# Seven inner products for two of the seven block products in a two-layer graph network

## The chip, the cores and the metric

The kernel runs on one core of one Trainium2 chip. A core has a matrix engine (TensorE, PE in the profile; its weight loads are PEld), three engines for elementwise work (VectorE or DVE, ScalarE or ACT, GpSimd or POOL), a queue engine (SyncE or SP) that issues the transfers, and 16 DMA engines. Every engine works through its own instructions in order; semaphores tie the engines together. The metric is the device time of one execution in microseconds. Before the change it is 2666.83 us, the median of three runs (2666.81 to 2668.23).

## What is computed

Two layers over 64 samples of 256 tokens with 512 features, in float32, all with the same 256x256 adjacency matrix:

```python
# layer 0: masked attention with 8 heads of 64, then residual and layer norm
q, k, v = x @ Wq + bq, x @ Wk + bk, x @ Wv + bv
scores = einsum('bqhd,bkhd->bhqk', q, k) / sqrt(64) + (1 - adj) * -1e9
x = layernorm(x + einsum('bhqk,bkhd->bqhd', softmax(scores), v) @ Wo + bo)
# layer 1: additive attention, then residual and layer norm
h = x @ W
e = leaky_relu((h @ a1)[:, :, None] + (h @ a2)[:, None, :], 0.2) * adj
x = layernorm(x + elu(softmax(e) @ h + beta * h))
```

## The kernel before

**Tiles.** The samples go in 32 pairs (`pair`, m = 0 to 31); q, k and v are made for both samples of a pair at once, all that follows for each sample s by itself (`batch`). Activations lie transposed, features on the 128 partitions, in four chunks of 128 features.

**Seven products.** A projection is cut into 2x2 blocks, and its eight block products are replaced by seven (Strassen's scheme in Winograd's form). `project` (line 435) issues them, in the order 1, 5, 2, 6, 3, 4, 7 for q, k and v of all pairs but the first. For q, k and v a block is 256 features by 256 features against 256 features by 256 tokens: four matmuls with 128x128 weights and 256 columns each. o and u have seven products of two such matmuls, spread (the second layer's attention times x) seven of two matmuls with 128 columns. The products gather in PSUM tiles (`ps_chain`, `ps_cross`, `ps_second`, `ps_fourth` or `ps_pair`); PSUM has eight banks. `gather` (line 490) brings them out: ScalarE copies the first product of a quarter (line 495, or 498 with a bias), VectorE adds the others onto it (line 504; for o, line 951).

**Sums of blocks.** The right-hand sums of tokens are GpSimd differences (`token_sums`, line 425; for spread, line 1083). Those of the weights are made once: for Wq and Wk by `streamed` (line 380), which puts them into DRAM and fetches each of the seven pieces again for every pair; for Wv, Wo and W they stay in SBUF (`weight_sums`, line 366).

**Attention.** `scores` (line 770) makes scores for two heads at a time, with 64-row weights, two matmuls side by side. VectorE adds the mask (line 786), ScalarE takes the exponential (line 788), GpSimd adds the two halves of the keys (line 791), VectorE transposes 32x32 blocks (line 797) and adds within them (line 798), which leaves four partial sums over keys. `denominators` (line 802) adds those four with one small matmul (`ps_den`, line 806), takes the reciprocal on VectorE (line 809), checks its range (line 811), and spreads it over all partitions through DRAM (lines 815 and 820). `mix` multiplies the weights with v, in two column halves (`ps_pv`, line 756); the result is divided on VectorE (line 873).

**Norm.** `norm` (line 584) takes the sum and the sum of squares on ScalarE (line 591), the root on GpSimd (lines 602 to 604), and scales on ScalarE (line 608). `finish` applies the elu on VectorE (lines 720 and 722).

**Order.** Nothing is issued where it is written. Each operation goes to a planner (`Plan`) with an assumed length, its buffers and what it reads and writes. TensorE's operations have a turn: `take_turn` (line 612) looks up the stage in `ROUND` and adds `LATER` to the pair's number, so that stages of several pairs interleave. The last pairs have an order written out, `FINISH`. `place` (line 127) keeps that order on TensorE and lays the other engines' operations by due time, with buffers counted in `slots`; it treats GpSimd and VectorE operations marked "two" as excluding each other. Every engine then runs the fixed order that results. In a middle period TensorE does: v, spread, scores, o, q, u, ps_den, mix, scores, k, spread, o, mix, ps_den, u.

## Time and profile before

| | |
|---|---|
| median of three runs | 2666.83 us |
| profiled execution | 2666.57 us |
| span of the profiled execution, first to last instruction | 2664.8 us |
| one period (a pair of samples) in the middle | 82.0 us |
| first matmul starts at | 3.75 us |
| last instructions behind the last matmul | 12.8 us |
| TensorE clock granted, mean | 0.998 of full speed |
| bytes from and to memory | 245.11 MB read, 52.48 MB written |
| DMA queue of the hardware, share of 16 engines | 42.1% |

In a row of the profile a line number says where the instruction stands in the kernel above, then come the engine, the operation, what it writes and reads, shapes (weights rows*columns for matmuls), and the count. A float32 matmul leaves two records. The lengths of matmuls are modelled; their starts are measured.

### The profile page before, as it was taken

The numbers are of one execution on the slowest core, as the hardware profiler recorded it, in microseconds if no ns is written. First come the engines' busy times: TensorE is split into PE (matmuls) and PEld (weight loads), VectorE is DVE, ScalarE is ACT, GpSimd is POOL, SyncE is SP. The second block draws the span as 40 slices with busy tenths as digits, with TensorE's granted clock in tenths as the row PEclk, the third lists the DMA queues.
The fourth block names the chain that finished last, engine by engine and source line by source line (L and its number), as shares of the span: only waits on it lengthen the run. The fifth ranks groups of instructions, "written<-read, shape, count | busy, mean of one in ns | idle before, by whom it ended". The sixth has DMA issues, their size and how long they took to land.

```text
span 2664.8 us, 45965 instructions
## 1 busy us (share of the span) xinstructions
PE 2643.7 (99%) x15037; PEld 2288.5 (86%) x15037; DVE 1999.7 (75%) x4053; ACT 1550.5 (58%) x3585; POOL 1637.5 (61%) x2255
## 2 busy tenths in 40 slices
PE   9999999999999999999999999999999999999998
PEld 7888888888888888888888888888888888888886
DVE  6677787777877777777778777787777777777876
ACT  3456565555655565655656555565556565565666
POOL 4665665655756556566566565575655656656655
PEclk9999999999999999999999999999999999999999
DMA  8343443444534434444344344453443444444321
GB/s 253 83 104 111 124 127 92 114 116 112 132 95 114 116 109 124 109 108 109 112 123 127 92 113 117 113 131 96 114 117 108 125 109 106 109 113 123 96 64 53
DMA packets 583084, 300.70 MB, mean 113 GB/s; under 512 B 409400, under 2 KB 513848, under 8 KB 582840
## 3 DMA queue, kind: packets, MB, share of 16 engines
q1 hardware_dynamic: 582712, 297.68, 42.1%
q8 instruction: 123, 2.02, 0.3%
q14 instruction: 121, 0.99, 0.1%
q0 software_dynamic: 128, 0.01, 0.0%
HBM read 245.11 MB, written 52.48 MB: 112 GB/s over the span
## 4 chain that ended last, share of the span: by engine, by line
PE 98%; DVE 0%; ACT 0%; DMA 0%; SPq 0%; issue 0%; POOL 0%; ACTq 0%; DVEq 0%
PE ps_chain L455 35%; PE ps_cross L455 23%; PE ps_sc L779 9%; PE ps_pv L756 9%; PE ps_pair L455 8%; PE ps_fourth L455 7%; PE ps_second L455 7%; PE ps_den L806 0%; DMA wq_sb<-in_L_gnn_Wq_dram 0%; ACT junk L591 0%; PE ps_plain L523 0%; DVE wq_sums_s L387 0%; DVE oT L873 0%; PE ps_y L1058 0%; PE ps_plain L518 0%; PE ps_plain L520 0%
## 5 line engine op out<-in xcount | busy, mean ns | idle before, releaser
L791 POOL TENSOR_TENSOR both<-pT 128x256 f32<-128x256 f32 x504 | 361.3, 742 | 55.9 <-ACT pT L788 55.8
L788 ACT ACTIVATE pT<-pT 128x512 f32<-128x512 f32 x512 | 307.0, 627 | 104.6 <-DVE pT L786 102.2
L602 POOL TENSOR_SCALAR rs<-sq 128x2 f32<-128x2 f32 (+1 forms) x130 | 25.4, 195 | 537.5 <-ACT junk L591 534.6
L591 ACT ACTIVATE junk<-x 128x512 f32<-128x512 f32 x256 | 159.7, 624 | 330.1 <-DVE x L951 311.8
L786 DVE TENSOR_TENSOR pT<-ps_sc,maskT_sb 128x512 f32<-128x512 f32 x512 | 319.7, 682 | 38.3 <-PE ps_sc L779 37.8
L1083 POOL TENSOR_TENSOR X_sums<-x 128x256 f32<-128x256 f32 x126 | 126.3, 1012 | 284.0 <-DVE x L720 211.6
L779 PE MATMUL ps_sc<-qT,kT 64*128 64x256 f32 x2048 | 240.2, 383 | 0.0
L756 PE MATMUL ps_pv<-pT,v 128*64 128x256 f32 x2048 | 238.1, 382 | 0.0
L779 PEld LDWEIGHTS ps_sc<-qT,kT 64*128 64x128 f32 x2048 | 193.2, 187 | 37.4 <-issue 12.2
L608 ACT ACTIVATE x<-x,nmr,rs 128x512 f32<-128x512 f32 x256 | 200.3, 807 | 31.5 <-POOL nmr L604 31.5
L756 PEld LDWEIGHTS ps_pv<-pT,v 128*64 128x64 f32 x2048 | 175.7, 137 | 44.3 <-issue 10.7
L974 DVE SCALAR_TENSOR_TENSOR junk<-x,wa_sb 128x512 f32<-128x512 f32 x256 | 173.9, 691 | 46.7 <-ACT x L608 46.6
L591 ACT ACTIVATE junk<-x,mean 128x512 f32<-128x512 f32 x256 | 182.8, 714 | 2.0
L797 DVE STREAM_TRANSPOSE flip<-both 128x512 f32<-128x512 f32 x252 | 176.8, 702 | 7.0 <-POOL both L791 0.5
L798 DVE TENSOR_REDUCE part<-flip 128x16 f32<-128x512 f32 x252 | 170.2, 676 | 3.2
L740 POOL TENSOR_TENSOR x<-x,res_sb 128x512 f32<-128x512 f32 x128 | 160.8, 1278 | 0.9 <-DMA x<-in_x_dram 0.9
L455 PE MATMUL ps_chain<-so_sb,oS 128*128 128x256 f32 x504 | 129.4, 379 | 0.0
L455 PE MATMUL ps_chain<-sw_sb,yS 128*128 128x256 f32 x504 | 129.4, 379 | 0.0
L951 DVE TENSOR_TENSOR x<-x,ps_chain 128x256 f32<-128x256 f32 x252 | 100.8, 411 | 28.9 <-PE ps_chain L455 27.8
L455 PE MATMUL ps_chain<-sv_sb,xS 128*128 128x256 f32 x512 | 120.9, 379 | 0.0
L425 POOL TENSOR_TENSOR oS<-oT 128x256 f32<-128x256 f32 x126 | 101.2, 803 | 30.8 <-DVE oT L873 23.1
L455 PE MATMUL ps_chain<-xS,wk_sums 128*128 128x256 f32 x496 | 117.2, 379 | 0.0
(246 smaller groups left out, 6985.2 us busy)
## 6 DMA issues: line engine op xcount, KB each, us to landing
x<-in_x_dram SPq DMA_DIRECT2D x64, 512.0 KB, 5.2
out_dram<-x SPq DMA_DIRECT2D x128, 256.0 KB, 2.9
inv_all<-rows SPq DMA_DIRECT2D x126, 256.0 KB, 4.1
xin<-in_x_dram SPq DMA_DIRECT2D x248, 128.0 KB, 3.2
wq_sums<-wq_sums SPq DMA_DIRECT2D x124, 256.0 KB, 3.4
wk_sums<-wk_sums SPq DMA_DIRECT2D x124, 256.0 KB, 2.6
wq_sums<-in_L_gnn_Wq_dram SPq DMA_DIRECT2D x93, 256.0 KB, 2.9
wk_sums<-in_L_gnn_Wk_dram SPq DMA_DIRECT2D x93, 256.0 KB, 2.7
```

The source lines that it names most:

```text
L455: nc.tensor.matmul(dst[:, f, :], lhs, rhs, start=start and f == 0 and c == 0, stop=c == inner - 1, skip_group_check=True)
L591: plan.op("ACT", ns, lambda: nc.scalar.activation(junk[A], X[:, t, :], func, accum_out=to[:, i:i + 1], **{k: v() if callable(v) else v for ...
L608: plan.op("ACT", 810, lambda i=i, t=t: nc.scalar.activation(X[:, t, :], X[:, t, :], AF.Identity, bias=nm[:, i:i + 1], scale=rs[:, i:i + 1] ...
L740: plan.op("POOL", 1300, lambda t=t: nc.gpsimd.tensor_tensor(X[:, t, :], X[:, t, :], res_sb[A], ALU.add), [res_sb], tokens(t))
L756: nc.tensor.matmul(acc[r * HD:(r + 1) * HD, i, :], V[:, 2 * k + s, h * HD:(h + 1) * HD], pT[h][:, k, :], start=k == 0, stop=k == NT - 1)
L779: nc.tensor.matmul(acc[j][:, k, :], kT[r:r + HD, c, key_blk(k)], own(qT, r, c), start=True, stop=True)
L786: plan.op("DVE", 680, lambda h=h, i=i: nc.vector.tensor_add(pT[h][A], acc[i][A], maskT_sb[A]), [acc[i], maskT_sb], [pT[h]])
L788: plan.op("ACT", 620, lambda h=h: nc.scalar.activation(pT[h][A], pT[h][A], AF.Exp, scale=1.0 / HD ** 0.5), [pT[h]], [pT[h]])
L791: plan.op("POOL", 735, lambda h=h, i=i: nc.gpsimd.tensor_tensor(both[c][:, i, :], pT[h][:, 0, :], pT[h][:, 1, :], ALU.add), [pT[h]], [(bot ...
L797: plan.op("DVE", 700, lambda: nc.vector.transpose(turned[A], both[c][A]), [both[c]], [turned])
L798: plan.op("DVE", 685, lambda: nc.vector.tensor_reduce(part[:, 2 * c:2 * c + 2, :], turned[A].rearrange("p i (q k) -> p i q k", k=32), AX.X ...
L974: plan.op("DVE", 770, lambda t=t, i=i, junk=junk: nc.vector.scalar_tensor_tensor(junk[A], X[:, t, :], 1.0, wa_sb[:, i, :], op0=ALU.mult, o ...
```

## The change

- **Inner products.** For all pairs but the first, products 2 and 4 of q, k and v are themselves cut into 2x2 blocks of 128x128 and made by seven matmuls with 128 columns, where there were four with 256. `inner_product` writes inner products 2, 3, 4 and 5 into the four quadrants of a PSUM tile, and 1, 6 and 7 into a second small one (`ps_inner`), to which 6 and 7 accumulate after the tile has been read. `add_part` adds the pieces to the quarters on VectorE: per product three additions of 128 columns and one of 256. `inner_sums` makes the token side of both, eight GpSimd differences of 128x128 a pair (`xQ`); the weight side is made once on GpSimd and streamed as two further pieces a projection.
- **Denominators.** The four partial sums come side by side by four DMAs, VectorE adds them (a reduction), takes the reciprocal of 64 columns and transposes it; the matmul goes, except for the last sample, which has its own.
- **Wv is streamed** like Wq and Wk, with nine buffers for pieces in place of six. In the first pair the token differences are on VectorE.
- **Order.** `ROUND`, `LATER` and `FINISH` are new, `START` writes out the first stages, k ahead of q; three matmuls on a constant stand first. A middle period on TensorE becomes: v, spread, o, u, k, mix, scores, q, spread, o, u, mix, scores.
- **Last pair.** The sum over features comes with the last addition of the elu (`accum_out`), and VectorE scales in ScalarE's place.

```diff
-ROUND = ("v", "x", "spread1", "scores20", "scores00", "scores10", "scores30", "o1", "logits0", "q", "logits1", "u1",
-         "sums0", "mix0", "scores11", "scores21", "scores01", "scores31", "attention0", "k", "spread0", "o0", "mix1",
-         "sums1", "u0", "attention1")
+ROUND = ("attention1", "v", "spread1", "attention0", "o1", "x", "u1", "k", "mix0", "scores01", "scores11", "scores21",
+         "scores31", "logits1", "q", "spread0", "o0", "u0", "logits0", "mix1", "scores00", "scores10", "scores20",
+         "scores30")
+LATER = {"scores00": -1, "scores10": -1, "scores20": -1, "scores30": -1, "scores01": 0, "scores11": 0, "scores21": 0,
+         "scores31": 0, "attention1": 2, "v": 0, "spread1": 2, "attention0": 1, "o1": 1, "x": -2, "u1": 2, "k": -1,
+         "mix0": 0, "logits1": 1, "q": -1, "spread0": 1, "o0": 0, "u0": 1, "logits0": 0, "mix1": 0}
...
+START = (("x", 0), ("k", 0), ("bias", 0), ("q", 0), ("x", 1), ("v", 0), ("mask", 0), ("scores10", 0), ("scores20", 0),
+         ("scores00", 0), ("scores11", 0), ("x", 2), ("scores30", 0), ("scores31", 0), ("mix0", 0), ("logits0", 0),
+         ("consts", 0), ("q", 1), ("scores21", 0), ("scores01", 0), ("v", 1), ("k", 1), ("mix1", 0), ("scores00", 1),
...
+DEEP = (2, 4)
...
-    slots = {"xin": 2, "x": 4, "two": 6, "xP": 1, "piece": 6, "full": 4, "half": 17, "flip": 1, "part": 1, "inv": 1,
-             "xS": 2, "st": 72, "ps": 8, "rows": 4, "svT": 4, "line": 4, "square": 4}
+    slots = {"xin": 2, "x": 4, "two": 6, "xP": 1, "piece": 9, "xQ": 2, "full": 4, "half": 19, "flip": 1, "part": 1, "inv": 1,
+             "xS": 2, "st": 72, "ps": 8, "rows": 4, "svT": 3, "line": 4, "square": 4}
...
+    busy(3)
...
+        inner = {}
+        for n in DEEP:
+            a = lambda f, c, n=n: w[:, 2 * raw[n][1] + c, (2 * raw[n][0] + f) * P:(2 * raw[n][0] + f + 1) * P]
+            I = sb("half", [4, P], f"{name}_i{n}")
+            for to, p, m, op, reads in (
+                    (0, (1, 0), (1, 1), ALU.add, [w]), (1, 0, (0, 0), ALU.subtract, [w, (I, 0)]),
+                    (2, (0, 0), (1, 0), ALU.subtract, [w]), (3, (0, 1), 1, ALU.subtract, [w, (I, 1)])):
+                plan.op("POOL", 455, lambda I=I, a=a, to=to, p=p, m=m, op=op: nc.gpsimd.tensor_tensor(
+                    I[:, to], *(a(*v) if isinstance(v, tuple) else I[:, v] for v in (p, m)), op), reads, [(I, to)])
...
+            if deep:
+                (raw_piece, reads), piece = fetch(n), sb("piece", [4, P], f"{name}_i{n}")
+                plan.op("SP", 370, lambda: nc.sync.dma_start(piece[A].rearrange("p k f -> p (k f)"), inner[n][A]),
+                        [inner[n]], [piece], lag=3900)
+                a = lambda f, c: (lambda: raw_piece()[:, c, blk(f)])
+                k = lambda i: (lambda: piece[:, i])
+                return [a(0, 0), a(0, 1), k(3), a(1, 1), k(0), k(1), k(2)], reads + [piece]
...
+            eng, ns = (nc.gpsimd, 180 + 545 * width // P) if engine == "POOL" else (nc.vector, 700)
+            plan.op(engine, ns, lambda: eng.tensor_tensor(dst(), p(), m(), ALU.subtract), reads, writes, mode="two")
...
+    def inner_sums(right, name):
+        r, keys = right
+        S = sb("xQ", [3, P], name)
+        b = lambda c, t: r()[:, c, t * P:(t + 1) * P]
+        ops = ((S, 2, (1, 1), (0, 1)), (None, (0, 1), (0, 1), (0, 0)), (S, 0, (1, 1), (0, 1)), (S, 1, (1, 0), 0))
+        for i, (buf, to, p, m) in enumerate(ops):
+            plan.op("POOL", 455, lambda to=to, p=p, m=m: nc.gpsimd.tensor_tensor(
+                *(b(*v) if isinstance(v, tuple) else S[:, v] for v in (to, p, m)), ALU.subtract),
+                keys + ([(S, 0)] if i == 3 else []), [(S, to)] if buf else keys)
+        b_, s_ = (lambda c, t: (lambda: b(c, t))), (lambda k: (lambda: S[:, k]))
+        return [b_(0, 0), b_(1, 0), b_(1, 1), s_(1), b_(0, 1), s_(0), s_(2)], keys + [S]
...
+        def inner_product(n, ks, to, start):
+            if n not in sums:
+                sums[n] = left(n, True)
+            reads = sums[n][1] + deep[n][1]
+            def pe():
+                for k in ks:
+                    f, t = {2: (0, 0), 3: (0, 1), 4: (1, 0), 5: (1, 1)}.get(k, (0, 0))
+                    l, r = sums[n][0][k - 1](), deep[n][0][k - 1]()
+                    dst = to[0][A] if to[0].shape == [P, P] else to[0][:, f, blk(t)] if by_feature else to[0][:, t, blk(f)]
+                    lhs, rhs = (l, r) if by_feature else (r, l)
+                    nc.tensor.matmul(dst, lhs, rhs, start=start and k == ks[0], stop=True, skip_group_check=True)
+            plan.op("PE", 224 * len(ks), pe, reads, [to], claims=claims)
+        def deep_four(n, whole, q, op):
+            inner_product(n, (2, 3, 4, 5), whole, True)
+            op(q, (whole, lambda: whole[0][A]))
+            add_part(q, (0, 1), (whole, lambda: whole[0][:, 1, P:2 * P]))
+            parts[n] = (ps([P], "ps_inner"), None)
+            inner_product(n, (1,), parts[n], True)
+            add_part(q, (0, 0), (parts[n], lambda: parts[n][0][A]))
+        def deep_six(n, q):
+            inner_product(n, (6,), parts[n], False)
+            add_part(q, (0, 1), (parts[n], lambda: parts[n][0][A]))
+        def deep_seven(n, q):
+            inner_product(n, (7,), parts[n], False)
+            add_part(q, (1, None), (parts[n], lambda: parts[n][0][A]))
+        if deep:
+            if 4 in deep:
+                deep_four(4, fourth, (1, 0), copy)
+            copy((0, 0), pe(1, chain, True))
+            if 2 in deep:
+                deep_four(2, second, (0, 0), add)
+            copy((1, 1), pe(5, cross, True))
+            if 4 in deep:
+                deep_six(4, (1, 0))
+            if 2 not in deep:
+                add((0, 0), pe(2, second, True))
+            copy((0, 1), pe(6, chain, False))
+            if 2 in deep:
+                deep_six(2, (0, 0))
+            if 4 in deep:
+                deep_seven(4, (1, 0))
+            add((0, 1), pe(3, cross, False))
+            if 4 not in deep:
+                copy((1, 0), pe(4, fourth, True))
+            if 2 in deep:
+                deep_seven(2, (0, 0))
+            acc = pe(7, chain, False)
+            add((1, 1), acc)
+            add((1, 0), acc)
+            return
...
+            def of():
+                return src() if t is not None else src().unsqueeze(1).to_broadcast([P, 2, P])
...
+            plan.op("DVE", 280 if t is not None else 410, both, [acc, key], [key])
...
+        if sums:
+            plan.op("DVE", 150, lambda: nc.vector.tensor_scalar(mean[A], sums[A], -1.0 / D, None, ALU.mult), [sums],
+                    [(mean, i) for i in range(n)])
...
+            if sums:
+                plan.op("DVE", 400, lambda i=i, t=t: nc.vector.tensor_scalar(
+                    X[:, t, :], X[:, t, :], rs[:, i:i + 1], nm[:, i:i + 1], ALU.mult, ALU.add),
+                    [nm, rs], [(X, (t, 0)), (X, (t, 1))], mode="two")
+                continue
...
+        elif (what, m) in START:
+            plan.turn = (-9, START.index((what, m)))
...
-        right = token_sums(xT, lambda k, j: [(xT, (j, s)) for s in range(2)], "xS", N)
+        right = token_sums(xT, lambda k, j: [(xT, (j, s)) for s in range(2)], "xS", N, "POOL" if m else "DVE")
+        deep = {n: inner_sums(right[n - 1], "xQ") for n in DEEP} if m else None
...
+            lv, left["v"] = streamed(wv_sb, Wv, "wv_sums")
...
-                turn("sums")
-                acc, inv = ps([32], "ps_den"), sb("inv", [32], "inv")
-                plan.op("PE", 80, lambda: nc.tensor.matmul(
-                    acc[0:P // 2], part[A].rearrange("p h q -> p (h q)"), fold_sb[A], start=True,
-                    stop=True), [part, fold_sb], [acc], mode="one", claims=[inv])
-                plan.op("DVE", 342, lambda: nc.vector.reciprocal(inv[0:P // 2], acc[0:P // 2]), [acc], [inv])
+                W, four = P // 4, sb("flip", [2, N], "four")
+                inv = sb("inv", [P // 2], "inv")
+                def gathered():
+                    return four[0:W, 0, :].rearrange("n (b c) -> n b c", b=4)
+                def fold():
+                    for b in range(4):
+                        nc.sync.dma_start(gathered()[:, b, :], part[b * W:(b + 1) * W].rearrange("n h q -> n (h q)"))
+                plan.op("SP", 1720, fold, [part], [(four, 0)], lag=2400)
+                plan.op("DVE", 330, lambda: nc.vector.tensor_reduce(
+                    inv[0:W], gathered().rearrange("n b c -> n c b"), AX.X, ALU.add), [(four, 0)], [inv])
+                plan.op("DVE", 200, lambda: nc.vector.reciprocal(inv[0:W], inv[0:W]), [], [inv])
                 for limit, op in ((SAFE, ALU.is_le), (1.0 / SAFE, ALU.is_ge)):
                     plan.op("DVE", 180, lambda limit=limit, op=op: nc.vector.scalar_tensor_tensor(
-                        fine_sb[0:P // 2], inv[0:P // 2], limit, fine_sb[0:P // 2], op0=op, op1=ALU.mult),
+                        fine_sb[0:W], inv[0:W], limit, fine_sb[0:W], op0=op, op1=ALU.mult),
                         [inv, fine_sb], [fine_sb], mode="two")
+                plan.op("DVE", 160, lambda: nc.vector.transpose(four[0:W, 1, 0:P // 2], inv[0:W]), [inv], [(four, 1)])
                 rows = Buf(dram_pool, "rows", [H, N], "rows")
                 plan.op("SP", 540, lambda: nc.sync.dma_start(
-                    rows[A].rearrange("h (q n) -> (h q) n", n=32), inv[0:P // 2]), [inv], [rows], lag=1700)
+                    rows[A].rearrange("h (q n) -> (h q) n", n=W).rearrange("(a j) n -> j a n", j=W),
+                    four[0:W, 1, 0:P // 2].rearrange("j (a n) -> j a n", n=W)), [(four, 1)], [rows], lag=1700)
...
```

## The prediction

> **What bounds the kernel now.** I read the page's busy shares and its chain of waits first, then TensorE's own timeline, then the busy time of every engine by stage.
>
> ```profile
> PE 2643.7 (99%) x15037; PEld 2288.5 (86%) x15037; DVE 1999.7 (75%) x4053; ACT 1550.5 (58%) x3585; POOL 1637.5 (61%) x2255
> PE 98%; DVE 0%; ACT 0%; DMA 0%; SPq 0%; issue 0%; POOL 0%; ACTq 0%; DVEq 0%
> ```
>
> TensorE is busy throughout, and 98% of the chain that ended last is TensorE's own work. A busy share alone would not do, since ends of matmuls are modelled; starts are not. So I take the price of a product from start to start. In the timeline (start, length, engine, line) the k products stand 1.73 us apart, the products of spread, half as wide, 0.45 us apart:
>
> ```profile
> 1045.94 1.89 PE L455 MATMUL ps_cross<-xT,wk_sums 128*128 128x256 f32 x8
> 1047.67 1.89 PE L455 MATMUL ps_second<-xT,wk_sums 128*128 128x256 f32 x8
> ...
> 1056.75 0.61 PE L455 MATMUL ps_cross<-attT,X_sums 128*128 128x128 f32 x4
> 1057.19 0.61 PE L455 MATMUL ps_second<-attT,x 128*128 128x128 f32 x4
> 1057.64 0.61 PE L455 MATMUL ps_chain<-att_sums,X_sums 128*128 128x128 f32 x4
> ...
> 1065.56 3.67 PE L756 MATMUL ps_pv<-pT,v 128*64 128x256 f32 x32
> 1069.07 0.25 PE L806 MATMUL ps_den<-fold_sb,part 128*64 128x32 f32 x2
> 1069.25 1.13 PE L455 MATMUL ps_chain<-w_sb,yT 128*128 128x256 f32 x4
> ```
>
> One 128x128 by 256 matmul (two records) costs 1.73/4 = 0.432 us, one with 128 columns 0.447/2 = 0.2235 us. Nothing stands between products, so a matmul taken out shortens the span, as long as nobody else becomes late. Busy time by stretch (start:end, length, then PE, PEld, DVE, ACT, POOL) shows who might: one whole period (a pair of samples) and, in it, a scores block and the o block after it.
>
> ```profile
> 1000.10:1082.10 82.00, 82.00 (x470) 71.32 (x469) 61.93 (x127) 48.38 (x112) 50.91 (x71) 1.00 0.42 113
> 1008.70:1012.40 3.70, 3.70 (x34) 3.05 (x33) 3.68 (x8) 1.56 (x3) 3.29 (x4) 1.00 0.74 119
> 1012.40:1018.50 6.10, 6.10 (x30) 5.41 (x29) 6.00 (x14) 3.35 (x6) 6.10 (x9) 1.00 0.67 105
> ```
>
> VectorE is full for 10 us after the scores and GpSimd nearly so, and TensorE still waits for neither: short backlogs are absorbed by spare PSUM banks. At the two ends of the run TensorE does wait; the largest wait is in the o product of the first sample (idle before it in brackets), with slow matmuls behind it:
>
> ```profile
> 89.72 2.00 PE L455 MATMUL ps_cross<-wo_sb,oT 128*128 128x256 f32 x4 [2.21 <-POOL oT L425]
> 91.52 1.89 PE L455 MATMUL ps_pair<-wo_sb,oT 128*128 128x256 f32 x4
> ```
>
> **The inner products.** In pairs 1 to 31 products 2 and 4 of q, k and v become seven products of 128x128 blocks with 128 columns. Before: 2 x 4 x 0.432 = 3.456 us a projection. After: 2 x 7 x 0.2235 = 3.129 us. That is 0.327 us, less than the eighth of 0.432 that the count of multiplications promises, because a narrow matmul costs more than half a wide one. 31 x 3 x 0.327 = **30.4 us** off TensorE.
>
> Here a rule of the Trainium skill speaks against the change: "TensorE: Matmul & The Clock Gate", section Back-to-back issue gap, says that in a stream of weight load and matmul pairs the spacing is set by both, about 81 ns a pass at 128 columns, where the stream alone would need 56. The row has two records 112 ns apart for one matmul, which at that page's rates are four passes of 56 ns. By the rule a narrow matmul would cost 0.324 us, fourteen of them 4.54 us, and the change would lose 31 x 3 x 1.08 = 100 us. Spread's products are the same shape and type, with new weights for every matmul, so I take the row.
>
> **Sums over keys, and the order.** The sums' matmul is small: in the rows above pv and ps_den together take 3.69 us from pv's start to u's. A pv block without one (at 2606.0 us, before the last sums' spread) takes 3.60, so it costs 0.08 us here, and by the same count 0.11 where it stands ahead of pv: 0.19 a pair. The new order puts pv and scores side by side twice a pair, where before one scores and one pv block stood alone: six changes of tile mode a period instead of seven, each 0.09 to 0.1 us (a 256-column record is followed after 0.31 us instead of 0.216). 32 x 0.19 + 31 x 0.095 = **9.0 us**. So a period falls from 82.0 to about 80.7 us.
>
> In exchange the denominators take four more DMAs out of SP's queue, a reduction, a longer reciprocal and a transpose. From scores to the mix that needs nothing of them and then to o lie more than half a period, some 40 us; two DMA round trips at the page's 1.7 to 4.1 us fit. Behind them in SP's queue stand weight pieces. SP issues some 20 more DMAs a pair (7 pieces of v, 6 inner pieces, 8 folds), at 0.3 to 0.7 us each about 10 us, on a queue that waits most of the time; the pieces' bytes add 13 x 256 KB to 9.3 MB a pair, DMA share from 0.42 to about 0.55. I cost both at nothing; if a piece came late, TensorE would wait for its landing, about 3 us.
>
> **VectorE and GpSimd.** Each inner-product pair of a projection adds six additions of 128 columns from PSUM and two of 256. A 128x512 one takes 682 ns, a 128x256 one 411, so 128 columns take about 276 (estimate by that slope). Per pair 18 x 0.276 + 6 x 0.411 = 7.4 us of durations; since back-to-back instructions overlap (512 x 682 ns of L786 are 319.7 us busy, 0.92), 6.8 us. The denominators add about 1.7 us: reciprocal of 64 columns 0.55 (344 ns for 32, 154 for 2), reduction 0.41, transpose 0.23, checks 0.44, against 0.72 a sample. 61.9 + 8.5 = 70.4 us of 80.7, 87%. GpSimd adds eight differences of 457 ns (median of att_sums), 3.7 us: 54.6 of 80.7, 68%.
>
> The mean hides a tight stage. By the order of instructions of the changed program, from a scores block to the end of the u after v (3.65 + 11.8 + 3.2 + 6.1 + 6.1 = 30.8 us) VectorE does 8 mask additions (5.5), 12 additions for v (2.7 + 2.5), 4 flips and 4 reductions (5.5), two oT (1.5), two L722 (1.5), L974, attT and svT (1.7), 16 additions for spread, o, u (6.6), denominators (1.2), two xT transposes (2.4) and L720 (1.4): 32.5 us, times 0.92 is 29.9, **97%**. The q half has about 27 of 34 us, so a backlog is paid back within the period. The skill's "SBUF — State Buffer", section SBUF: two separate sides, says the port pair is an exclusive lock between GpSimd and a VectorE instruction with two SBUF inputs. The trace agrees (L387 on VectorE 1628 ns in the crowded start, 694 alone), so the oT and L722 instructions of that stage can each be held for one GpSimd instruction, 0.73 us. By the rows alone VectorE just keeps up; with the lock taken against it four times it ends some 3 us late, and the second inner accumulation of v, which I find about 0.5 us early, would wait. TensorE's new waits: between nothing and 2 us a pair. Nearest is the scores-o stage shown above, 98% full and without a wait; I take 0.15 us a pair, **+5 us**.
>
> GpSimd's closest date is xS and xQ (one xS buffer): after v's last product it does 4 of 1.28, 7 of 0.73 and 7 of 0.457, about 13.5 us, and k needs them 15.3 + 0.45 us later. No two-input VectorE work lies in that window, so 2 us remain.
>
> **Start and end.** The written order moves the first o to where its sums are long done: the block that took 10.37 us takes 6.15, and 0.73 before it goes, **-4.9**. Three warm-up matmuls run while x is fetched; q's first product took 3.2 us instead of 1.73 partly for a slow clock: **-1.5** (0 to -2.5). The scores that waited 0.85 us for the transposes do no longer. Against that, the first k product now finds VectorE with four token differences, bv_wo and kT ahead of the weight sums, and GpSimd with 24 differences that hold the port: +3 (1 to 6). Six scores in a row with the mix at once behind them: ten mask additions of 0.682 and an exp of 0.63 end about 2 us after TensorE gets there, +2. New pieces are first written, then read: +1 (0 to 4). Together **-1.2**. At the end the sum over features comes with the last addition and normalizing is done on VectorE, so 0.81 us of L591 become about 0.15 and 0.81 us of L608 about 0.48 (L544): **-1.0** of the 12.8 us behind the last matmul.
>
> **Sum.** 2664.8 - 30.4 - 9.0 - 1.2 - 1.0 + 5 = 2628.2 us of span. The profiled execution took 2666.57, 1.8 more than its span, and the median is 2666.83, 0.3 above it: **2630 us**. Its own range is 2617 to 2644. A measurement can tell 0.2% (5 us) from no change.
>
> **Rivals.** (1) VectorE is late now and then: waits of 0.8 us a pair instead of 0.15 leave half the gain, about 2650. For it the 97%, against it the 98% above that cost nothing. (2) Slower: in the v stage VectorE and GpSimd hold each other up in every period, and v's inner accumulations wait 2 us: 31 x 2 = 62 us against a gain of 41.6, about 2687. It decides from 1.3 us a pair. For it that both engines gained work and lost time, and that its instructions stand in a fixed order, so that one held by the port holds all behind it; against it that a backlog under 1 us is hidden by banks. A gap of 2.2 us also cost 2 us of half-speed clock at 89.7 us; gaps this small did not. (3) Narrow matmuls behave as the rule says, 2630 + 130 = 2760: hardly with the row at hand. (4) The reduction of work is real but v's pieces arrive late and eat it: within 5 us of before.
>
> **Chances.** Likeliest 0.66; (1) 0.16; (4) 0.05; (2) 0.11 and (3) 0.01 on the slow side; a bigger gain, below 2615, 0.01. Faster 0.83, same 0.05, slower 0.12. The range that leaves out no more than two in ten runs from a little under the likeliest case's lower end to rival (1)'s upper end: 2615 to 2662.
>
> **What would show it.** Right: a period of about 80.7 us from one k block to the next; inner products' matmuls 0.2235 us apart; VectorE near 87% and GpSimd near 68% in a middle period; no ps_den but the last sample's; the o block of the first sample at 6.15 us. Wrong: TensorE gaps before inner accumulations released by VectorE's part additions or oT, gaps before k's first products released by GpSimd's xQ, gaps released by weight pieces, or a start longer than 5 us of waits.

## The result, and the profile after

The changed kernel takes **2694.43 us** (median of four runs, 2691.39 to 2697.82), where the kernel before took 2667.44 beside it (2666.81 to 2668.23). The ratio is 1.0101, with a 95% interval of 1.0084 to 1.0119: it is slower by 27 us, where 37 us faster was forecast. The time lies outside the range and on the other side.

The page of the changed kernel, its busy shares and the chain that ended last, by engine and by line:

```profile
PE 2628.0 (98%) x16033; PEld 2243.8 (83%) x16033; DVE 2210.2 (82%) x4942; ACT 1503.8 (56%) x3573; POOL 1743.7 (65%) x2519
PE 73%; DMA 10%; DVE 10%; SPq 3%; issue 3%; ACT 1%; POOL 0%; DVEq 0%; POOLq 0%; ACTq 0%
PE ps_chain L515 25%; PE ps_cross L515 15%; PE ps_pv L918 8%; PE ps_sc L941 7%; PE ps_pair L515 6%; PE ps_inner L545 4%; DMA four<-part 4%; PE ps_fourth L545 3%; PE ps_second L545 3%; SPq L974 2%; DMA wv_sums_i<-wv_sums 2%; DVE xT L809 1%; DVE pT L948 1%; PE ps_fourth L515 1%; DVE inv L977 1%
```

TensorE is busy 15.7 us less than before, and yet the span is 28.6 us longer. The chain, which was 98% TensorE's, now leaves it for a quarter of the time, and the largest name in it beside TensorE's is the denominators' transfer `four<-part` with its issue on SP (line 974); the reduction that reads it (line 977) is there too.

One period in the middle (start:end, length, then PE, PEld, DVE, ACT and POOL busy, clock, DMA share, GB/s) against the prediction's 80.7 us, 70.4 us of VectorE, 54.6 of GpSimd and a DMA share of 0.55:

```profile
1043.40:1126.20 82.80, 80.72 (x498) 69.27 (x497) 68.17 (x154) 46.37 (x113) 54.65 (x79) 1.00 0.57 153
```

The loads are as forecast; only the length isn't. The prices are too. At the end of this period, in TensorE's timeline, the inner products' matmuls stand 0.22 us apart:

```profile
1126.19 0.39 PE L545 MATMUL ps_fourth<-xS,wk_sums_i 128*128 128x128 f32 x2
1126.42 0.39 PE L545 MATMUL ps_inner<-xS,wk_sums 128*128 128x128 f32 x2
1126.64 1.68 PE L515 MATMUL ps_chain<-xT,wk_sums 128*128 128x256 f32 x7
```

So the time went between the instructions. Start to start on TensorE, in us per block, between 150 and 2500 us (the sum counts k, q, v once, the rest twice a pair, as the period does):

| | before, mean | after, median | after, mean |
|---|---|---|---|
| k, q, v together | 36.37 | 35.58 | 35.88 |
| spread | 3.17 | 3.13 | 3.28 |
| o | 6.14 | 6.05 | 6.29 |
| u | 6.14 | 6.45 | 6.73 |
| scores | 3.65 | 3.65 | 3.65 |
| pv, with the sums' matmul before | 3.70 | 3.60 | 3.63 |

In a pair where nothing is late the period is 80.62 us, as forecast; in the mean it is about 2.2 us more. More than half of that lies in u, which takes 6.09 us (mean of its two) in that undisturbed pair. Here is one u, as TensorE, SP and VectorE went through it (start, length, engine, line; in brackets the idle time before and its releaser):

```profile
1119.78 1.03 PE L515 MATMUL ps_chain<-sw_sb,yS 128*128 128x256 f32 x4
1120.64 1.03 PE L515 MATMUL ps_cross<-sw_sb,yT 128*128 128x256 f32 x4
1123.72 1.10 PE L515 MATMUL ps_pair<-w_sb,yS 128*128 128x256 f32 x4 [2.05 <-DVE four L984]
```

```profile
1107.97 1.33 SPq L453 DMA_DIRECT2D wk_sums<-wk_sums  x3
1109.40 0.38 SPq L900 DMA_DIRECT2D x<-in_x_dram  x1
1109.87 0.42 SPq L453 DMA_DIRECT2D wk_sums<-wk_sums  x1
1110.34 0.58 SPq L1170 DMA_DIRECT2D line<-svT  x1
1115.67 0.32 SPq L1172 DMA_DIRECT2D row<-line  x1
1116.08 2.50 SPq L974 DMA_DIRECT2D four<-part  x4
```

```profile
1113.19 0.66 DVE L960 TENSOR_REDUCE part<-flip 128x16 f32<-128x512 f32 x1
...
1117.39 0.75 DVE L1123 TENSOR_TENSOR x<-x,ps_chain 128x256 f32<-128x256 f32 x2 [0.44 <-PE ps_chain L515]
1119.99 0.59 DVE L977 TENSOR_REDUCE inv<-four 32x64 f32<-32x256 f32 x1 [1.84 <-DMA four<-part]
1120.51 1.22 DVE L809 STREAM_TRANSPOSE xT<-xin 128x1024 f32<-128x1024 f32 x1
1121.66 0.50 DVE L979 RECIPROCAL inv<-inv 32x64 f32<-32x64 f32 x1
1122.09 1.18 DVE L809 STREAM_TRANSPOSE xT<-xin 128x1024 f32<-128x1024 f32 x1
1123.20 0.37 DVE L623 TENSOR_TENSOR u<-ps_pair,u 128x256 f32<-128x256 f32 x1
```

Read it backwards. TensorE waits for the PSUM bank of `ps_pair`, whose last user is the addition `u<-ps_pair` at 1123.20. (The profile names `four` at line 984, which ends at that moment; but in all 29 such gaps the matmul starts 0.15 us behind the addition's end, also in the one where another instruction follows it.) That addition stands in VectorE's fixed order behind the reduction at line 977, and VectorE stood idle for 1.84 us in front of it; of TensorE's 2.05 us that is nearly all. The reduction waited for the four fold DMAs. Their data was there at 1113.85, but SP issued the first only at 1116.08, because in SP's own order `row<-line` stands ahead, and that one waited 4.75 us for `line` to land. `line` holds 1 KB, but SP had issued 1.5 MB just ahead of it, four pieces of weights of 256 KB each and 512 KB of x. The waits of the whole run, VectorE's at the reduction and TensorE's behind it (total, times, longest):

```profile
DVE inv L977 <- DMA four<-part: 51.1, 52, 3.1
PE ps_pair L515 <- DVE four L984: 25.0, 28, 2.1
```

This is a reading, not yet a cause. The experiments have to tell whether that stand is what costs the time, or whether VectorE is simply too full, or whether it is the new order as a whole.

### The profile page after: what moved, and what is told of

It reads as the page before. It is cut to its first block, busy times and chain, and to the rows that moved or that the text cites. A ratio compares the mean times of both kernels' runs of the same rounds, so it can differ in the third digit from the quotient of the medians.

```text
span 2693.4 us, 50162 instructions
## 1 busy us (share of the span) xinstructions
PE 2628.0 (98%) x16033; PEld 2243.8 (83%) x16033; DVE 2210.2 (82%) x4942; ACT 1503.8 (56%) x3573; POOL 1743.7 (65%) x2519
## 3 DMA queue, kind: packets, MB, share of 16 engines
q1 hardware_dynamic: 666184, 408.06, 56.1%
q14 instruction: 138, 1.13, 0.1%
## 4 chain that ended last, share of the span: by engine, by line
PE 73%; DMA 10%; DVE 10%; SPq 3%; issue 3%; ACT 1%; POOL 0%; DVEq 0%; POOLq 0%; ACTq 0%
PE ps_chain L515 25%; PE ps_cross L515 15%; PE ps_pv L918 8%; PE ps_sc L941 7%; PE ps_pair L515 6%; PE ps_inner L545 4%; DMA four<-part 4%; PE ps_fourth L545 3%; PE ps_second L545 3%; SPq L974 2%; DMA wv_sums_i<-wv_sums 2%; DVE xT L809 1%; DVE pT L948 1%; PE ps_fourth L515 1%; DVE inv L977 1%
## 5 line engine op out<-in xcount | busy, mean ns | idle before, releaser
L953 POOL TENSOR_TENSOR both<-pT 128x256 f32<-128x256 f32 x504 | 382.3, 781 | 66.7 <-ACT pT L950 64.4
L918 PEld LDWEIGHTS ps_pv<-pT,v 128*64 128x64 f32 x2048 | 141.8, 137 | 87.1 <-issue 22.2
L1255 POOL TENSOR_TENSOR X_sums<-x 128x256 f32<-128x256 f32 x126 | 99.5, 800 | 168.6 <-ACT x L757 81.1
L757 ACT ACTIVATE x<-x,nmr,rs 128x512 f32<-128x512 f32 x252 | 194.7, 809 | 7.8 <-POOL nmr L748 6.2
L1146 DVE SCALAR_TENSOR_TENSOR junk<-x,wa_sb 128x512 f32<-128x512 f32 x256 | 192.1, 752 | 0.2 <-ACT x L757 0.2
L1184 POOL TENSOR_TENSOR e<-e,adj_sb 128x512 f32<-128x512 f32 (+1 forms) x66 | 93.2, 1413 | 147.2 <-DVE e L1181 146.0
L1040 ACT COPY oT<-ps_pv 128x512 f32<-128x512 f32 x128 | 74.3, 581 | 119.8 <-PE ps_pv L918 118.8
L614 ACT COPY yT<-ps_chain 128x256 f32<-128x256 f32 x126 | 46.5, 369 | 157.3 <-PE ps_chain L515 157.3
```

The source lines that it names most:

```text
L757: plan.op("ACT", 810, lambda i=i, t=t: nc.scalar.activation(X[:, t, :], X[:, t, :], AF.Identity, bias=nm[:, i:i + 1], scale=rs[:, i:i + 1] ...
L918: nc.tensor.matmul(acc[r * HD:(r + 1) * HD, i, :], V[:, 2 * k + s, h * HD:(h + 1) * HD], pT[h][:, k, :], start=k == 0, stop=k == NT - 1)
L953: plan.op("POOL", 735, lambda h=h, i=i: nc.gpsimd.tensor_tensor(both[c][:, i, :], pT[h][:, 0, :], pT[h][:, 1, :], ALU.add), [pT[h]], [(bot ...
L1146: plan.op("DVE", 770, lambda t=t, i=i, junk=junk: nc.vector.scalar_tensor_tensor(junk[A], X[:, t, :], 1.0, wa_sb[:, i, :], op0=ALU.mult, o ...
```

## The experiments

All ran with three timing rounds against the kernel before, which took 2666.6 to 2666.9 us beside them. In `plan.op` the word `lag` is the planner's assumption of how long after its issue a transfer has landed; changing it leaves the work the same and moves only the planned order. Where "waits" of TensorE are told, they are start-to-start times above the usual one for these shapes, summed over a stretch from 0.12 us up, at a single place in full.

### Two ways around the stand

**A second flip buffer.** `four`, which takes the folded sums, shares one buffer with the transposes of the next scores.

```diff
-"half": 19, "flip": 1
+"half": 18, "flip": 2
```

> The changed kernel with two flip buffers and 18 of half, nothing else: the control for the run with matmul sums, and a test of theory F (the fold's target four takes the only flip buffer, so flips and folds wait for each other). Theories D and L: 2690 to 2700, as the changed kernel. Theory F: below 2675.

Measured: **2660.77 us**, ratio 0.998 (0.9972 to 0.9988). That is theory F's number. But with a second buffer the planner also lays another order (over half of the places in VectorE's order hold another instruction than in the changed kernel), so the run does not tell the buffer from the order. The stand shrinks to a third:

```profile
DVE inv L977 <- DMA four<-part: 16.5, 31, 1.7
```

**A later planned reduction**, with the one buffer kept:

```diff
-                plan.op("SP", 1720, fold, [part], [(four, 0)], lag=2400)
+                plan.op("SP", 1720, fold, [part], [(four, 0)], lag=4500)
```

> The changed kernel with 4500 ns in place of 2400 ns assumed for the landing of the fold DMAs, so that the planner lays the reduction and the reciprocal later on VectorE; the work is the same. Theory D: most waits behind L977 go: 2645 to 2670. Theory L: 2690 to 2700.

Measured: **2660.87 us**, ratio 0.9977 (0.9966 to 0.9987), with 8.9 us of stand in place of 51.1. Two edits with nothing in common but that stand give back the same 34 us, and VectorE's work is untouched in both. That speaks against theory L, VectorE's load: a VectorE that was too full would have stayed so.

**The fold ahead of `row<-line` on SP.** Taking `line` to land 5.0 us behind its issue (in place of 1.9) lets the planner put the fold first in SP's order at that place.

```diff
-                line[A].rearrange("(t g j) -> g t j", t=NT, j=32), svT[0:P:32]), [svT], [line], lag=1900)
+                line[A].rearrange("(t g j) -> g t j", t=NT, j=32), svT[0:P:32]), [svT], [line], lag=5000)
```

> The changed kernel with one planned landing changed: the line of features is taken to land 5.0 us behind its issue instead of 1.9, so that in each pair the fold of the weight sums stands ahead of row<-line in SP's order, and no longer behind its wait. One flip buffer. Theory Q (it is SP's in-order queue: the fold is issued about 2 us late because row<-line in front of it waits for line's landing): the waits at the reduction fall from 1.8 to below 0.5 us a pair and the time to 2660 to 2675. Theory B (it is the one flip buffer, which the next transposes share with the fold's target): 2685 to 2700.

Measured: **2683.72 us**, ratio 1.0065 (1.0048 to 1.0082). Half a confirmation: the stand at the reduction falls to 14.8 us in 21 and the wait in front of u's product 4 (the sixth in order) from 31.8 to 12.3 us, as theory Q has it, but the time is nearer to theory B's. New waits stand elsewhere: q's inner products 10.4 us, and a single gap of 7.7 us in front of a spread product. So the stand can be cured with one buffer, but each new order costs something of its own, and with that the three runs above can't say what the stand alone is worth.

### The stand alone, every order unchanged

Here each engine's order is that of the changed kernel, instruction for instruction (but for one memset at the start), and all DMAs are issued. Only what the reduction reads is changed, a constant in place of the folded sums, so that it has nothing to wait for. The true denominators are thereby left out.

```diff
-                    inv[0:W], gathered().rearrange("n b c -> n c b"), AX.X, ALU.add), [(four, 0)], [inv])
+                    inv[0:W], still[0:W].rearrange("n (b c) -> n c b", b=4), AX.X, ALU.add), [(four, 0)], [inv])
```

> The changed kernel, every engine's order the same, all DMAs issued; only the reduction of the folded sums reads a constant tile instead of the fold's target, so that it waits for no DMA (the attention's weights are then scaled by a constant: that part of the computation is left out). Theory D (VectorE's stand at the reduction is the loss): the waits for a reused bank before u's fourth product, 31.8 us, go, and 2655 to 2668. Theory O (the order as a whole, with its other waits, is the loss): above 2680.

Measured: **2661.66 us**, ratio 0.9981 (0.9974 to 0.9989). The wait in front of u's product 4 falls from 31.8 to 8.2 us (none above 0.3), that in front of o's products from 9.5 to nothing, that in front of q's inner products rises from 5.8 to 13.8; in all, 33 us of time are gone. This shows the cause without a new order: VectorE's stand for the fold's landing is worth 33 us, and with it the change's sign. Port conflicts of GpSimd and VectorE, the mechanism of rival (2), are not the cause of these 33 us, since all their instructions are still there.

It also shows that the stand isn't the whole miss: 2662 is still 32 us above the forecast. TensorE's page of waits in this run:

```profile
PE ps_inner L545 <- DVE qT L642: 12.6, 16, 1.9
PE ps_chain L515 <- ACT yT L614: 3.9, 11, 0.8
```

q's last inner products wait for a narrow addition, and in VectorE's order the transpose `attT` (line 1219) stands ahead of that addition, waiting for another round trip through DRAM. It did so before the change too, but there no wait of TensorE followed:

```profile
DVE attT L1219 <- DMA att_b<-square: 34.9, 27, 2.9
DVE attT L1047 <- DMA att_b<-square: 24.5, 30, 1.7
```

The first line is this run's, the second the kernel's before. So the next run takes that wait away as well (the attention of the second layer is left out too):

```diff
-            plan.op("DVE", 675, lambda: nc.vector.transpose(attT[A], att_b[A]), [att_b], ...
+            plan.op("DVE", 675, lambda: nc.vector.transpose(attT[A], diag_sb[A]), [att_b], ...
```

> As e13, and the transpose attT reads a constant tile as well instead of att_b (the attention of the graph layer is then a constant matrix: left out too); every order the same. Theory Q (what is left of TensorE's waits comes from VectorE standing at attT for att_b): another 8 to 15 us less than e13. Theory V (what is left comes from how full VectorE and GpSimd are): within 4 us of e13.

Measured: **2659.53 us**, ratio 0.9976 (0.9967 to 0.9986): theory V's number. q's wait is gone, and another has come in its place:

```profile
PE ps_chain L515 <- ACT yT L614: 23.3, 19, 3.4
```

The seven products of spread now wait for ScalarE's copies out of PSUM, in the stage right behind q. What is won at q is lost a few microseconds later. (The profiled execution took 2670.75 us, the longest of fourteen, so in the median one these waits are smaller.) The trace shows what makes ScalarE late. In its own fixed order `z` (line 1175) stands ahead of those copies and waits for `row`, the third round trip through DRAM. Before the change it hardly did, as the second line shows:

```profile
ACT z L1175 <- DMA row<-line: 118.8, 30, 6.7
ACT z L1003 <- DMA row<-line: 2.4, 1, 2.4
```

All 24 waits of TensorE at this place in the middle of the run, 27.8 us, come right behind such a stand; so do the 13 of the changed kernel, 7.4 us. No run took this stand away.

### What the inner products are worth

With two flip buffers, with and without inner products (`DEEP = ()`, so that q, k and v have seven products of 256 columns as before):

```diff
-DEEP = (2, 4)
+DEEP = ()
```

> The changed kernel with two flip buffers (half slots 18) and q, k, v by seven products of 256 columns as before the change (no inner products). The prediction gives the inner products 3 x 0.327 us a pair, 30.4 us in all; the records of after say 3 x 0.22. Theory W (the work is really saved, undiminished by new waits): 2660.8 + 20 to + 31, so 2681 to 2692. Theory N (the inner products' waits for narrow additions and pieces eat what they save): 2655 to 2668.

Measured: **2661.96 us**, ratio 0.9986 (0.9978 to 0.9994), against 2660.77 with them. Theory N. Yet the work saved is real. With the same stage in front of each, a k block takes 12.180 us without and 11.853 with inner products, a q block 12.191 and 11.865: 0.327 and 0.326, the forecast's 0.327 to the digit. Of the 30 us, 27 are found again as waits: those of TensorE are 13.9 us without inner products (4.7 at the start, 8.4 in the middle, 0.8 at the end) and 40.7 with them (14.6, 23.3, 2.8).

Of the share at the start, 5.9 us lie in the first k block, which has no inner products (19.21 us with, 13.29 without; 15.48 in the changed kernel). Another part lies in the second pair, the first with inner products. In the changed kernel its q takes 15.61 us, its v 14.83 and its k 12.29, where the blocks later take 11.86: 7.1 us. The gaps wait for pieces of weights and for narrow additions. So in the next run that pair goes without:

```diff
-        deep = {n: inner_sums(right[n - 1], "xQ") for n in DEEP} if m else None
+        deep = {n: inner_sums(right[n - 1], "xQ") for n in DEEP} if m and m > 1 else None
```

> Two flip buffers, and the inner products begin with the third pair instead of the second (the second pair's q, k, v by products of 256 columns, so 3 blocks more at about 0.31 us, +0.9 us). With two flip buffers TensorE waited 14.6 us in the first 100 us, without inner products 4.7. Theory S (the inner sums and their pieces are late only for the second pair): 2651 to 2656. Theory G (the waits at the start come from making the weights' inner sums, whoever uses them first, and move with them): 2659 to 2664.

Measured: **2656.41 us**, ratio 0.9966 (0.9957 to 0.9974), 4.4 us better than with two flip buffers alone. Theory S misses its upper edge by 0.4 us, theory G is out by more. The waits did not move on: the second pair's blocks take 12.2 to 12.3 us, and the third pair's are no longer than with two flip buffers alone (k 13.30 against 13.29, q 14.64 against 15.17). This is the fastest kernel of the study, 0.34% ahead of the kernel before: a saving of some 38 us of work comes out as 10.

### Planned landings nearer to the measured ones

If stands for transfers are the trouble, better assumptions should help further. Four runs say that they don't by themselves.

The edits of the first three runs together, and two lengths as measured:

```diff
-"half": 19, "flip": 1    ... [(four, 0)], lag=2400)    ... [line], lag=1900)
+"half": 18, "flip": 2    ... [(four, 0)], lag=4500)    ... [line], lag=5000)
-plan.op("DVE", 330, lambda: nc.vector.tensor_reduce(    ... plan.op("DVE", 200, lambda: nc.vector.reciprocal(
+plan.op("DVE", 590, lambda: nc.vector.tensor_reduce(    ... plan.op("DVE", 500, lambda: nc.vector.reciprocal(
```

> The changed kernel's work, unchanged, with a second flip buffer (half slots 19 to 18), the fold planned to land 4.5 us behind its issue instead of 2.4, the line of features 5.0 instead of 1.9, and the inverse's reduction and reciprocal planned at 590 and 500 ns instead of 330 and 200. Theory D (VectorE stands in its fixed order for late landings, nothing else is wrong): periods of 80.6 us become the rule, middle waits of TensorE fall below 41 us, so 2640 to 2662. Theory L (the two cures of before took the same 34 us and what is left is VectorE's load): no better than 2661, or worse if the longer planned waits push other work.

Measured: **2672.01 us**, ratio 1.002 (1.0006 to 1.0033). Theory D misses. Theory L's words leave room for the number, but VectorE's load is that of the runs at 2661 us; what differs is the order. VectorE's stand has moved to `attT`:

```profile
DVE attT L1219 <- DMA att_b<-square: 52.3, 28, 2.8
PE ps_inner L545 <- DVE qT L642: 19.1, 23, 1.5
```

Next, with two flip buffers, `square`, the transfer ahead of `att_b`:

```diff
-                square[A].rearrange("(t p) j -> p t j", p=P), e[A]), [e], [square], lag=2400)
+                square[A].rearrange("(t p) j -> p t j", p=P), e[A]), [e], [square], lag=4500)
```

> Two flip buffers, and square (the attention's way to memory) taken to land 4.5 us behind its issue instead of 2.4; it landed after a median 4.7 us there. att_b<-square and the transpose attT behind it are planned later. Theory Q (VectorE's order has another instruction, attT, standing for a late landing ahead of q's last additions, which costs 7 us in q's last inner products and 10 us in the product over the attention's sums): those two waits fall below 6 us together and the time to 2645 to 2655. Theory R (each new order brings waits of its own, of about the same size): 2656 to 2672.

Measured: **2686.37 us**, ratio 1.0076 (1.0059 to 1.0092). The stand at `attT` falls to 10.3 us, and the one at the reduction is back, this time ahead of the additions of o:

```profile
DVE inv L977 <- DMA four<-part: 58.0, 49, 2.5
PE ps_cross L515 <- DVE x L1123: 25.6, 24, 1.9
```

The same with the inner products from the third pair on (`if m and m > 1`):

> Two flip buffers, inner products from the third pair, and square at 4.5 us: all three. Theory Q with S: 2638 to 2650, ahead of every kernel so far. Theory R with G: 2656 to 2672.

Measured: **2682.70 us**, ratio 1.0062 (1.0044 to 1.0079). The 3.7 us of the second pair are won here too, the rest stays.

And the fastest kernel with the fold planned later:

```diff
-                plan.op("SP", 1720, fold, [part], [(four, 0)], lag=2400)
+                plan.op("SP", 1720, fold, [part], [(four, 0)], lag=3500)
```

> Two flip buffers, inner products from the third pair on, and the fold taken to land 3.5 us behind its issue instead of 2.4. Theory Q (planned landings near the measured ones leave fewer stands): 2645 to 2656. Theory R (each new order brings waits of its own): 2656 to 2680.

Measured: **2663.15 us**, ratio 0.9986 (0.9977 to 0.9995). All four are slower than the kernel they start from. In the first three a new order removes one stand and puts another in front of something that TensorE needs, as theory R says, though two of the times lie above its 2672. What the last one loses stays open: its profiled execution took 2653.94 us, the fastest of twelve, so the trace does not show the loss.

### The denominators without the inner products, and the reverse

**Before, with the denominators by DMA alone**: `denominators` (lines 802 to 820) is that of the changed kernel.

```diff
-                turn("sums")
-                acc, inv = ps([32], "ps_den"), sb("inv", [32], "inv")
...
+                W, four = P // 4, sb("flip", [2, N], "four")
+                inv = sb("inv", [P // 2], "inv")
...
+                plan.op("SP", 1720, fold, [part], [(four, 0)], lag=2400)
...
-             "xS": 2, "st": 72, "ps": 8, "rows": 4, "svT": 4, "line": 4, "square": 4}
+             "xS": 2, "st": 72, "ps": 8, "rows": 4, "svT": 3, "line": 4, "square": 4}
```

> The kernel before with the denominators by DMAs alone (fold, reduction, transpose on VectorE instead of the matmul; three svT buffers instead of four, for room). VectorE has 75% load there. Theory D: VectorE stops at L977 here too and TensorE waits where an addition is behind it: 2675 to 2700. Theory L: VectorE has room, the sums' matmul is saved: 2658 to 2668.

Measured: **2783.24 us**, ratio 1.0431 (1.0413 to 1.0448), 116 us slower. Theory D had the sign and less than a third of the size. The reduction's stand is only 21.0 us there; larger is the idle time at the next link of the same route, where the multiplication with the spread inverse (`oT`, line 880 in this kernel) waits for its landing and for ScalarE. That this is what costs the 116 us is a reading; no run tried it. Of the oT group's page line (busy, mean; idle time ahead and its releasers):

```profile
L880 DVE TENSOR_TENSOR oT<-oT,inv_all 128x512 f32<-128x512 f32 x126 | 82.4, 689 | 175.0 <-ACT oT L875 84.1 <-DMA inv_all<-rows 67.2 <-ACT junk L588 18.3
```

**After, with the sums by a matmul again**: `denominators` is that of the kernel before, in mix's turn, with two flip buffers.

```diff
-                W, four = P // 4, sb("flip", [2, N], "four")
-                inv = sb("inv", [P // 2], "inv")
...
+                turn("mix")
+                acc, inv = ps([32], "ps_den"), sb("inv", [32], "inv")
+                plan.op("PE", 80, lambda: nc.tensor.matmul(
+                    acc[0:P // 2], part[A].rearrange("p h q -> p (h q)"), fold_sb[A], start=True,
...
-"half": 19, "flip": 1
+"half": 18, "flip": 2
```

> The changed kernel with the partial sums added by the small matmul again, as before the change, ahead of the mix; everything else as changed, but two flip buffers in place of one and 18 buffers of half in place of 19, without which the first pairs' order can't be laid out. Theory D (VectorE stands still at the reduction L977 until the four fold DMAs have landed, and holds the additions behind it, which TensorE waits for): the 42 us of waits behind such stops go, some 10 us of matmul and mode changes come back: 2645 to 2665. Theory L (VectorE is too full as a whole, 82% and 97% in the stage of v): only 1.7 us a pair of VectorE's work goes, so 2685 or more.

Measured: **2882.65 us**, ratio 1.0809 (1.0791 to 1.0827); more than 200 us above theory D's range, and by a mechanism that neither theory had. VectorE stands at `attT` (line 1212 in this kernel), and q's inner products wait for the addition behind it:

```profile
DVE attT L1212 <- DMA att_b<-square: 181.4, 29, 7.5
PE ps_inner L548 <- DVE qT L645: 162.4, 28, 7.3
```

In SP's timeline of one such pair `inv_all<-rows`, waiting 3.5 us for `rows` to land, stands ahead of the four `att_b<-square`. It is the same figure with other names. Three runs try to take it away.

```diff
-                    rows[A].rearrange("h (q n) -> (h q) n", n=32), inv[0:P // 2]), [inv], [rows], lag=1700)
+                    rows[A].rearrange("h (q n) -> (h q) n", n=32), inv[0:P // 2]), [inv], [rows], lag=3500)
```

> As the run with the sums over keys by a matmul (2882.65 us), with one planned landing changed: rows<-inv is taken to land 3.5 us behind its issue instead of 1.7, which puts att_b<-square ahead of inv_all<-rows in SP's order. Theory Q (that run lost its time because att_b was issued behind inv_all's wait for rows, VectorE stood at attT for it and q's additions stood behind): 2660 to 2690, about 9 us over the run with two flip buffers (2660.8), by the 9.0 us that the prediction gives the matmul and its mode change. Theory M (the matmul on TensorE and its place cost the time): above 2850.

`att_b` goes ahead: **2776.00 us**, ratio 1.0405 (1.0387 to 1.0422). 107 us are won, which leaves the time between the two theories, and 135.6 us of stand at `attT` remain, now for `square`.

Then `square` at 4.5 us as well (`[square], lag=4500`):

> The sums over keys by a matmul again (two flip buffers, rows 3.5 us as in the run before), and square taken to land 4.5 us behind its issue instead of 2.4, where VectorE had stood 135.6 us at attT. Theory Q (that stand is the loss): VectorE's stand at attT below 40 us and 2670 to 2710. Theory M (the matmul's place in this round of turns, whatever the landings): above 2750.

Measured: **2828.56 us**, ratio 1.0608 (1.0582 to 1.0634). That is theory M's number. The stand at `attT` is gone, and q still waits 105.9 us.

Last, the order of the first of these runs kept, with `attT` reading a constant as above (`diag_sb` for `att_b`):

> The run with the sums over keys by a matmul that took 2882.65 us, every order the same; only the transpose attT reads a constant tile instead of att_b (the graph attention is a constant: left out). Theory Q (the stand at attT is that run's loss): 2660 to 2700. Theory M (the matmul's place in this round of turns, whatever VectorE waits for): above 2800.

Measured: **2809.41 us**, ratio 1.0537 (1.0518 to 1.0556). 73 us are won; the rest moves to VectorE's transposes, which wait for GpSimd's sums ahead of q's additions:

```profile
DVE flip L962 <- POOL both L956: 107.8, 59, 4.5
```

Theory Q explains a third of that run's loss; the time is theory M's. **What the denominators' two ways are worth against each other stays open**: in no order that was run does the matmul's version go without large waits of another origin.

## Why the prediction was wrong, step by step

- **Inner products, -30.4 us: right** as work: 0.327 us a block forecast, 0.326 and 0.327 measured. The row of spread's products was the right price, and the 81 ns a pass of the Trainium skill ("TensorE: Matmul & The Clock Gate", Back-to-back issue gap) the wrong one for these matmuls.
- **Sums over keys and tile modes, -9.0 us: right** as work. The undisturbed period is 80.62 us, forecast 80.7.
- **"From scores to the mix that needs nothing of them … two DMA round trips … fit … I cost both at nothing": the step that failed.** The denominators did arrive in time for the mix; that part holds. But the question was who stands in the queues while they travel. The reduction that waits for the fold stands in VectorE's one order ahead of u's addition, and the fold's issue stands on SP behind another wait. The prediction listed the weight pieces behind the fold on SP, but neither what stood ahead of it (`row<-line`, waiting for a landing that itself came behind 1.5 MB of other transfers) nor what stood behind its reader. Price: 33 us in place of nothing, by the run with every order unchanged.
- **TensorE's new waits, 0.15 us a pair, +5 us: far too small** even without that stand. In the run in which the reduction waits for nothing the blocks' mean times add up to 81.85 us a pair, 1.2 above the undisturbed period: 13.8 us in front of q's inner products, behind the stand at `attT`, 6.5 in spread, behind the stand at `z`, and 8.2 in front of u's product 4. The first two are two more round trips through DRAM whose readers stand ahead of what TensorE needs; that they cost this much is read from the trace, since the run that took one of them away only enlarged the other. I read the scores-o stage, 98% full and without a wait, as proof that short backlogs cost nothing. With more instructions on VectorE, a late one has more behind it.
- **Start, -1.2 us: parts right, one mis-sized.** First k: 15.48 us against 12.19 usually, +3.3 (forecast +3). First o: 6.24 us (forecast 6.15). First matmul at 0.93 us, and the full clock granted from 6.2 us on in place of 11.3. The mix behind the six scores hardly waits (forecast +2). But the second pair's three blocks, for which the sum has only "new pieces are first written, then read: +1 (0 to 4)", took 7.1 us more than usual: TensorE stood idle there for 2.8 us in front of pieces, within that range, and for 2.1 in front of inner products that waited for narrow additions, which the sum left out.
- **End, -1.0 us: right.** 11.8 us behind the last matmul, 12.8 before.
- **Loads: right.** VectorE 68.2 us in the period shown (forecast 70.4), GpSimd 54.65 (54.6), DMA share 0.57 (0.55). The reduction of the fold took 0.59 us (0.41), the reciprocal 0.50 (0.55), the last transpose 0.23.
- **Rivals.** Rival (2) had nearly the time, 2687, by the wrong mechanism; its words "stand in a fixed order, so that one held … holds all behind it" were the right ones, with the port in the place of a DMA's landing. Rival (1), 0.8 us a pair and 2650, comes nearest to what is left when the stand is cured (1.2 us and 2662). What the port costs in that rest was not tested; GpSimd's `both` took 781 ns in the mean, 742 before.

Together, of the 65 us between 2628.2 and the span of 2693.4: 33 for the stand; 1.2 us a pair of further waits, some 35 in the middle against 5 in the sum; and 6 more in the second pair. That makes 69, 4 more than are missing, about as well as mean block times can tell.

## What to carry to other kernels

An in-order engine pays for a wait with everything that stands behind it, so a transfer that "fits" before its result is needed is still not free: look at what follows its first reader on that engine, and at what precedes its issue on the queue, waits and bytes alike. A DMA's reader belongs behind the last instruction that the bottleneck engine needs soon, or on an engine with nothing of the kind, and its target in a buffer of its own. When a kernel runs at 98% of its bottleneck, work taken off that engine is only worth what the others' order allows: here about 38 us of work gave 10 at best.

## What the runs showed of the hardware

- **A small transfer landed late when much had been issued just ahead of it.** From the end of `line`'s issue (1 KB) to the issue that stood for it, in the changed kernel: median 1.29 us (1.13 to 2.13) in the 29 cases where SP had issued 256 KB in the 3 us ahead, 4.76 us (4.36 to 5.18) in the 26 with 1.5 MB. Before the change, mostly with nothing issued ahead, the median was 1.10 us and the most 2.2. The mean load does not explain it: with two flip buffers the DMA share was 58.0% (56.1% in the changed kernel) and `line` landed after a median 1.25 us in the 23 cases with 256 KB ahead. No run changed the bytes ahead alone. The fold's last issue to the reduction that stood for it took a median 2.7 us, at most 4.1.
- **Times spread more.** 41 executions of the kernel before lie between 2664.6 and 2669.2 us (0.17%), 20 of the fastest one between 2650.8 and 2670.1 (0.7%). A period that waits on transfers takes over their unevenness; that is an inference, no run separates it.
- **TensorE's clock fell behind gaps of about 2 us, but not always.** In the traces of all eighteen kernels, without the first 20 and the last 60 us, none of 88 idle gaps of 1.0 to 1.5 us was followed by a stretch of half the granted clock, 2 of 27 at 1.5 to 1.8 us, 22 of 33 at 1.8 to 2.6, 38 of 43 at 2.6 to 3.5 and all 72 above. Such a stretch lasted 3.4 us, or two or three times that. In the changed kernel three of the five gaps of 1.9 to 2.1 us were followed by one; its mean clock stayed at 0.997. In the run with the sums by a matmul, with gaps of some 7 us, 186 matmul records behind them stood about 0.21 us further apart than usual (0.43 in place of 0.22), some 39 us in all, at a mean clock of 0.961.
